# Loading the first two chunks of W and base one by one, with VectorE's first steps reordered and two warm-up products instead of five

## The chip, the core and the metric

The kernel runs on one core of a Trainium2 chip. A core has TensorE (PE, matrix products; its weight loads are listed as PEld), VectorE (DVE), ScalarE (ACT), GpSimd (POOL) and SyncE (SP), which run side by side and wait for each other through semaphores. In this kernel SP issues the loads. Sixteen DMA engines carry out every load and store. The metric is the device time of one execution in microseconds (us).

## The reference

Eight batches of x (1024 x 512 each) pass two layers with residual connections. Both are steered by a row of cond (8 x 512).

```python
# layer 0, D = 512, RANK = 8
ae = layernorm(cond) * ln_g + ln_b
h  = gelu(ae @ w1 + b1)
xw = h @ w2 + b2                       # w2: 512 x 8192
x_a, x_b = halves of xw, each reshaped to (8, 512, 8)
layer = base_layer + einsum('bdr,bkr->bdk', x_a, x_b)
x = x + (x + x @ layer)                # per batch
# layer 1
ys = cond / sqrt(512)
d  = rsqrt(ys**2 @ weight**2 + 1e-8)
x  = x + ((x * ys) @ weight) * d
```

Both layers are linear in x for a given batch, so the kernel multiplies the two matrices first and then x by the product: for batch b, with W = `weight`, P_b = (2I + base + rank part) times (I + ys W d). Float32 accuracy is reached by splitting each matrix into a rounded upper part (h) and a rest (l) and adding three products: h·h, h·l and l·h.

## The kernel before

The work has three stages. First a prologue: cond's normalisation, the layer-1 scale d, and the first matrix product (batch 0: base times W scaled by ys, tiles `pg`). Then a setup stage in which the low-rank part is made: `w2` is streamed in as sixteen tiles of 1024 KB (`w2_group`, tiles `w`, products `px` on PE), mixed with the base products of batches 1 to 3 (tiles `pq`). Then the main stage, in which each batch's x is multiplied by its matrix (tiles `po`), with the matrices of later batches made in between (tiles `pp`).

A matrix of 512 rows lies in SBUF as four chunks k of 128 rows, 128 partitions x 4 x 512. The order on PE, ACT, DVE and SP in the prologue and the setup stage is written out by hand: `mm` and `turn` pin PE's instructions, and the wrappers `ve`, `se` and `sy` pin those of DVE, ACT and SP to the order in which the code names them. So a line that moves in the code moves in the engine's queue.

The pieces that the change touches:

- Lines 86 to 92, SP's first loads: `sm` (small constants, the identity, cond transposed), cond, then W and base in two halves, then w1. In the trace these loads are `w_sb<-in_weight` (W), `b_raw<-in_baseT` (base) and `w_sb<-in_w` (this is w1; its tile's name is shortened to another's). Behind them on SP stand the w2 tiles, with consts (`cst`) after the first of them; the rows `condrows` and `b2rows` and the matrix `b_nat` come later in the stream. At most nine tiles of the pool `big` exist at a time, so a later w2 tile's load waits until PE has used up an earlier one. DMA semaphores are used in turn, eight of them, so a load also waits for the landing of the one eight before it.
- `round_yw(k)`: ACT writes the upper part of chunk k of ys·W into `nh`. `rest_yw(k)`: DVE writes the rest into `nl`.
- `twice_i(k)`: DVE adds 2I to a 128 x 128 block of base chunk k. `round_b(k, lo, hi, by)`: the upper part of columns lo to hi of base chunk k into `bh`, by ACT or, for the block of chunk 0 that `twice_i` changed, by DVE. `rest_b(k)`: DVE writes the rest into `bl`.
- `square_w(k)`: ACT squares W's chunk into `wsq`, for the products `pq_v`, from which d comes.
- `keep_warm(count)`: PE multiplies zeros by zeros, with no use of the result; 12 at the start (`WARM`), and 5 more on line 256, after the four turns of ae (`pa`) and before the first twelve products of `pg`.

After line 256 PE runs chunk 0's twelve products (four of bh·nh, four of bh·nl, four of bl·nh), then chunk 1's for two of the four tiles `pg`, then `pq_v`, then chunk 1's other two, and so on. The eleventh `w2_group` on PE stands on line 753, behind the turns `pb` of `rank_t`.

Of the kernel before, what the change touches and what calls it, by code (L numbers as in the profile page):

```python
# [14 lines left out]
P = 128  # L15
NB = 8
NT = 1024
D = 512
# [12 lines left out]
def cond_resid_kernel(ctx: ExitStack, tc: tile.TileContext, small, cond, condrows, consts,  # L31
# [12 lines left out]
    def mm(*args, **kw):  # L44
        tc.keep_in_program_order(nc.tensor.matmul(*args, **kw))  # L45

    def turn(*args):
        tc.keep_in_program_order(nc.tensor.transpose(*args))
# [36 lines left out]
    cnd, ae, xab, drow = scr[:NB, 0, :], scr[:NB, 1, :], scr[:, 2, :], scr[:, 3, :]  # L85
    sy.dma_start(sm, small)
    sy.dma_start(cnd, cond)
    for at in (slice(0, 2), slice(2, 4)):
        sy.dma_start(w_sb[:, at, :], weight[:, at, :])
        sy.dma_start(b_raw[:, at, :], baseT[:, at, :])  # L90
    w1_sb = big_tile("w1_sb")
# [14 lines left out]
    def keep_warm(count):  # L106
        for _ in range(count):
            mm(warm.rearrange("p (a c) -> p a c", c=P), zero,
               zero.unsqueeze(1).to_broadcast([P, D // P, P]), start=True, stop=True)
# [29 lines left out]
    def round_yw(k):  # L139

        se.mul(n0[k][0], w_sb[:, k, :], ysT[:, k, 0:1])

    def rest_yw(k):
        h, l = n0[k]
        ve.scalar_tensor_tensor(l, w_sb[:, k, :], ysT[:, k, 0:1], h.bitcast(F32),
                                           ALU.mult, ALU.subtract)

    def twice_i(k):
        blk = b_raw[:, k, k * P:(k + 1) * P]
        ve.scalar_tensor_tensor(blk, ident, 2.0, blk, ALU.mult, ALU.add)  # L150

    def round_b(k, lo=0, hi=D, by=se.copy):
        (by(bh[:, k, lo:hi], b_raw[:, k, lo:hi]))

    def rest_b(k):
        ve.tensor_sub(bl[:, k, :], b_raw[:, k, :], bh[:, k, :].bitcast(F32))
# [26 lines left out]
    rstd = sp.tile([NB, 1], F32, name="rstd")  # L183
    ve.tensor_mul(rstd, r, t)
    ve.tensor_scalar(ae, cnd, mv[:, 0:1], rstd, ALU.subtract, ALU.mult)
    round_yw(1)
    twice_i(0)
    round_b(0, 0, P, ve.tensor_copy)
    round_b(0, P, D)
    twice_i(1)  # L190
    round_b(1)
    rest_yw(0)
    rest_b(0)
    rest_yw(1)
    rest_b(1)
    for k in range(KC):
# [56 lines left out]
    pa = misc.tile([P, KC, NB], F32, tag="misc", name="pa")  # L253
    for k in range(KC):
        turn(pa[:, k, :], ae[:, k * P:(k + 1) * P], ident[:NB, :NB])
    keep_warm(5)
    for i, (s, m) in enumerate(((bh, n0[0][0]), (bh, n0[0][1]), (bl, n0[0][0]))):
        for c in range(KC):
            mm(pg[c], s[:, 0, c * P:(c + 1) * P], m, start=(i == 0), stop=False)
# [679 lines left out]
```

## Time and profile before

| What | Value |
|---|---|
| Median of 4 runs | 304.24 us (304.16 to 304.5) |
| Profiled execution, in all | 304.26 us |
| Its span | 302.3 us |
| PE busy | 296.1 us, 98% of the span |
| DVE busy / ACT busy / POOL busy | 177.6 / 145.6 / 34.9 us |
| Granted PE clock over the span | 0.999 |
| Bytes moved | 62.11 MB, mean 205 GB/s |
| W's two loads, issue to landing (shortest, longest) | 4.0 and 6.9 us |
| base's two loads, issue to landing (shortest, longest) | 4.9 and 7.7 us |

Times in the trace count from the start of the span. A line of the timeline or of the chain gives a start, a duration, the engine, the line of the code and what is written and read; a bracket at the end tells how long the engine sat idle before and what it waited for. Since helpers record nearly every instruction, most have line 45 (PE) or 62 (the others), and one goes by the names of tiles. A line of the stage table gives the stretch, its length, then busy time and count for PE, PEld, DVE, ACT and POOL, the granted clock, the DMA engines' busy share and GB/s. A line of the list of waits gives the waiting engine and tile, what it waited for, the sum, the number and the longest, in us.

### The profile page before, as it was taken

How to read it: one execution, taken by the hardware profiler on the slowest of the kernel's cores; microseconds unless marked ns; L12 is line 12 of the kernel's file. 1: busy time of each engine (PE TensorE's matmuls, PEld its weight loads, DVE VectorE, ACT ScalarE, POOL GpSimd, SP SyncE). 2: the span in 40 equal slices, each digit the busy share in tenths (PEclk: the TensorE clock that was granted, in tenths of full speed). 3: DMA queues.
4: the chain of work that ended last, by engine and by line, in shares of the span. 5: the costliest groups of instructions: out<-in, count | busy, mean ns of one | idle time of the engine just before them, and what ended most of it. 6: DMA issues, size and time to landing. Idle time of an engine off the chain costs nothing.

```text
span 302.3 us, 3652 instructions
## 1 busy us (share of the span) xinstructions
PE 296.1 (98%) x1369; PEld 223.4 (74%) x1369; DVE 177.6 (59%) x263; ACT 145.6 (48%) x212; POOL 34.9 (12%) x74
## 2 busy tenths in 40 slices
PE   8999999999999999999999999999999999999995
PEld 3655465466878778888888877888888878888884
DVE  4779840979569889793157549993365268500000
ACT  4756132256566672673366534664464456521221
POOL 0011000057014504100000027000000000000000
PEclk9999999999999999999999999999999999999999
DMA  6999999596519977186134348524254253522222
GB/s 203 407 430 415 407 428 415 206 329 182 194 69 324 324 244 257 72 255 211 57 112 167 112 180 207 197 88 192 60 202 184 77 208 88 228 104 104 104 85 92
DMA packets 19218, 62.11 MB, mean 205 GB/s; under 512 B 2800, under 2 KB 3312, under 8 KB 14848
## 3 DMA queue, kind: packets, MB, share of 16 engines
q1 hardware_dynamic: 6064, 38.78, 34.6%
q10 hardware_dynamic: 9360, 16.78, 14.8%
q0 software_dynamic: 3776, 6.31, 7.5%
q8 instruction: 11, 0.18, 0.3%
q14 instruction: 7, 0.06, 0.1%
HBM read 44.02 MB, written 17.84 MB: 205 GB/s over the span
## 4 chain that ended last, share of the span: by engine, by line
PE 86%; DMA 5%; DVE 5%; ACT 2%; issue 1%; SPq 0%; ACTq 0%
PE po L45 58%; PE pp L45 13%; PE pq L45 7%; DMA w<-in_w 4%; PE px L45 3%; PE pg L45 2%; DVE n L62 2%; DMA b_raw<-in_baseT 2%; PE pr L45 1%; PE pt_t L45 1%; ACT work L62 1%; DVE scr L62 0%; PE ps_t L45 0%; DVE q L62 0%; SPq L62 0%
## 5 line engine op out<-in xcount | busy, mean ns | idle before, releaser
L45 PE MATMUL po<-ph,xs 128*128 128x512 f32 (+1 forms) x520 | 165.0, 388 | 0.0
L45 PEld LDWEIGHTS po<-ph,xs 128*128 128x128 f32 x520 | 97.2, 188 | 21.5 <-issue 1.7
L45 PE MATMUL po<-pl,xs 128*128 128x512 f32 (+1 forms) x260 | 100.4, 386 | 0.0
L62 ACT COPY o<-po 128x512 f32<-128x512 f32 (+1 forms) x65 | 37.7, 580 | 85.3 <-PE po L45 85.3
L45 PEld LDWEIGHTS po<-pl,xs 128*128 128x128 f32 x260 | 48.9, 188 | 9.8
L62 DVE TENSOR_TENSOR xs<-x,xs 128x1024 fp32r<-128x1024 f32 x32 | 38.9, 1222 | 18.7 <-ACT xs L62 18.7
L62 ACT CAST xs<-x 128x1024 fp32r<-128x1024 f32 x32 | 33.4, 1053 | 3.5 <-DMA x<-in_x 3.0
L62 DVE TENSOR_TENSOR nl_p<-n,nh_p 128x1024 fp32r<-128x1024 f32 x14 | 17.1, 1223 | 23.1 <-ACT nh_p L62 23.0
L62 DVE TENSOR_TENSOR q<-pr,q 128x512 f32<-128x512 f32 x32 | 20.1, 686 | 7.0 <-PE pr L45 7.0
L509 POOL DMA_DIRECT2D fa<-kept_a x28 | 13.8, 516 | 77.3 <-PE pr L45 77.1
L62 DVE TENSOR_TENSOR pl<-q,ph 128x1024 fp32r<-128x1024 f32 x16 | 19.3, 1221 | 1.1 <-ACT ph L62 1.0
L45 PE MATMUL pq<-nh,bh 128*128 128x512 f32 x48 | 19.8, 412 | 0.0
L45 PE MATMUL pq<-nl,bh 128*128 128x512 f32 x48 | 19.1, 397 | 0.1
L45 PE MATMUL pq<-nh,bl 128*128 128x512 f32 x48 | 18.9, 394 | 0.0
L62 ACT COPY q<-pp 128x512 f32<-128x512 f32 x20 | 11.8, 588 | 14.1 <-PE pp L45 13.3
L62 DVE SCALAR_TENSOR_TENSOR n<-w_sb,ysT,d 128x512 f32<-128x512 f32 x24 | 17.8, 749 | 0.9 <-DMA d<-d_out 0.9
L62 ACT CAST ph<-q 128x1024 fp32r<-128x1024 f32 x16 | 16.6, 1052 | 3.4 <-DVE q L62 3.1
L62 ACT CAST nh_p<-n 128x1024 fp32r<-128x1024 f32 x14 | 14.7, 1052 | 3.5 <-DVE n L62 1.9
L45 PE MATMUL px<-w,hT 128*32 128x512 f32 x128 | 16.0, 601 | 0.2 <-DMA w<-in_w 0.2
L45 PEld LDWEIGHTS pq<-nh,bh 128*128 128x128 f32 x48 | 9.0, 188 | 8.4 <-issue 5.0
L509 POOL DMA_DIRECT2D ft<-kept_t x28 | 13.8, 523 | 5.0 <-DMA kept_t<-st_t 5.0
L45 PE MATMUL pp<-nh_p,sh 128*128 128x512 f32 x32 | 12.4, 389 | 0.0
(139 smaller groups left out, 285.9 us busy)
## 6 DMA issues: line engine op xcount, KB each, us to landing
w<-in_w SPq DMA_DIRECT2D x16, 1024.0 KB, 10.8
x<-in_x SPq DMA_DIRECT2D x16, 1024.0 KB, 5.3
out<-o ACTq DMA_DIRECT2D x63, 256.0 KB, 2.0
ft<-kept_t POOLq DMA_DIRECT2D x28, 64.0 KB, 3.1
fa<-kept_a POOLq DMA_DIRECT2D x28, 64.0 KB, 3.1
d<-d_out POOLq DMA_DIRECT2D x6, 256.0 KB, 3.8
w_sb<-in_weight SPq DMA_DIRECT2D x2, 512.0 KB, 5.5
b_raw<-in_baseT SPq DMA_DIRECT2D x2, 512.0 KB, 6.3
```

The lines of the kernel that those rows point to most:

```text
L45: tc.keep_in_program_order(nc.tensor.matmul(*args, **kw))
L62: return lambda *a, **kw: pin(f(*a, **kw)) if InOrder.on else f(*a, **kw)
L509: nc.gpsimd.dma_start(fold[name, b][32 * c:32 * c + 32, :], kept[name, g][32 * i:32 * i + 32, :])
```

## The change

W and base's chunks 0 and 1 are loaded by four DMAs of 256 KB (W 0, base 0, W 1, base 1) instead of two of 512 KB; chunks 2 and 3 stay together. On ACT the rounding of base chunk 0 moves ahead of that of W chunk 1. On DVE the two rests of chunk 0 move ahead of `twice_i(1)`. Of the zero products on line 256 two are left.

```diff
-    for at in (slice(0, 2), slice(2, 4)):
+    for at in (slice(0, 1), slice(1, 2), slice(2, 4)):
         sy.dma_start(w_sb[:, at, :], weight[:, at, :])
         sy.dma_start(b_raw[:, at, :], baseT[:, at, :])
...
-    round_yw(1)
+    round_b(0, P, D)
     twice_i(0)
     round_b(0, 0, P, ve.tensor_copy)
-    round_b(0, P, D)
+    round_yw(1)
+    rest_yw(0)
+    rest_b(0)
     twice_i(1)
     round_b(1)
-    rest_yw(0)
-    rest_b(0)
     rest_yw(1)
     rest_b(1)
...
-    keep_warm(5)
+    keep_warm(2)
     for i, (s, m) in enumerate(((bh, n0[0][0]), (bh, n0[0][1]), (bl, n0[0][0]))):
```

## The prediction

> **What bounds the kernel now.** I read the page's engine shares first, then the chain of work that ended last, then the waits of TensorE (PE), then the two places that these name.
>
> ```profile
> PE 296.1 (98%) x1369; PEld 223.4 (74%) x1369; DVE 177.6 (59%) x263; ACT 145.6 (48%) x212; POOL 34.9 (12%) x74
> ...
> PE 86%; DMA 5%; DVE 5%; ACT 2%; issue 1%; SPq 0%; ACTq 0%
> ```
>
> PE is busy for 98% of the span, so time can come only from places where PE waits. The list of PE's waits has four rows:
>
> ```profile
> PE warm L45 <- DVE eps_l L62: 1.0, 1, 1.0
> PE pd L45 <- DVE dst L62: 0.5, 1, 0.5
> PE pg L45 <- DVE bh L62: 0.4, 1, 0.4
> PE px L45 <- DMA w<-in_w: 0.2, 1, 0.2
> ```
>
> Row 3 is the place that the change works on. The chain over the first 12 us shows what stands before it: the load of base chunks 0 and 1, two VectorE (DVE) steps, then the products of pg.
>
> ```profile
> 1.99 4.88 DMA b_raw<-in_baseT
> ...
> 6.89 0.30 DVE b_raw L62
> ...
> 7.22 0.24 DVE bh L62
> 7.46 0.14 issue
> 7.60 4.44 PE pg L45 x18
> ```
>
> Row 4 looks harmless at 0.2 us, but it is a second gate. The chain between 30 and 50 us and PE's timeline there:
>
> ```profile
> 37.03 10.89 DMA w<-in_w
> 47.92 0.04 issue
> 47.96 1.07 PE px L45 x8
> ```
> ```profile
> 47.11 0.66 PE L48 MATMUL pb<-sm,work 128*128 128x128 f32 x4
> 47.96 1.07 PE L45 MATMUL px<-w,hT 128*32 128x512 f32 x8 [0.20 <-DMA w<-in_w]
> ```
>
> PE is ready at 47.76 and the eleventh w2 tile lands at 47.92. A transfer of 1024 KB that takes 10.89 us stands in a queue, and the stage table shows a full one:
>
> ```profile
> 2.50:4.50 2.00, 2.00 (x6) 0.72 (x5) 1.45 (x7) 0.29 (x1) 0.00 (x0) 1.00 0.86 203
> 4.50:6.00 1.50, 1.50 (x10) 0.66 (x9) 0.89 (x4) 0.36 (x1) 0.00 (x0) 1.00 0.99 396
> 6.00:7.70 1.70, 1.28 (x6) 0.46 (x7) 0.77 (x4) 1.42 (x4) 0.00 (x0) 1.00 1.00 267
> 12.00:20.00 8.00, 8.00 (x51) 4.94 (x54) 4.77 (x18) 4.62 (x10) 0.75 (x2) 1.00 1.01 422
> ...
> 40.00:45.00 5.00, 5.00 (x30) 2.72 (x29) 1.86 (x3) 1.95 (x4) 0.00 (x0) 1.00 1.02 424
> ```
>
> The last two columns are the DMA engines' busy share and GB/s. The trace's landing records agree. Each load ends on its slowest DMA engine: W chunks 0-1 at 5.62, base 0-1 at 6.87, W 2-3 at 9.36, base 2-3 at 10.61, w1 at 13.07, the first w2 tile at 15.58; and at the end the ninth w2 tile at 40.48, the tenth at 42.96, b_nat at 45.45, the eleventh at 47.92. The late steps are 2.47 to 2.49 us, which is eight packets of 8 KB at their 309 ns: that engine never rests. From 13.07 to 47.92 are 34.85 us: twelve such tiles (11 w2 and b_nat, 29.8), consts 0.36, condrows 0.65, b2rows 1.27, the d rows 1.4 and one instruction fetch about 1.35, together 34.8. There is no hole in it. So the gate at 47.92 is set by the bytes queued ahead of it, not by when PE frees a tile.
>
> **Part 1: the loads.** W chunk 0 lands earlier, as 256 KB instead of 512. Its first packet should start at 2.57 as now. W's packets of 4 KB averaged 278 ns between 2.5 and 4.5 us (base's, from 4.5 to 6.0, 163). Half the bytes are 1.1 us, and the tail to landing is now about 0.8 (5.62 less 2.57 less eight packets at 278), so W chunk 0 lands at about 4.5. Base chunk 0 is eight packets of 2 KB at 85 ns (the median of the 2 KB packets in this trace): 5.2 instead of 6.87. W 1 and base 1 land at about 6.3 and 7.0.
>
> The price: 32 packets of 2 KB per DMA engine take the place of 16 of 4 KB. At 85 against 159/2 ns that is 32 x 5.5 = 0.18, taken as 0.2 us, on a queue without holes, so everything behind lands 0.2 later, the eleventh w2 tile too. SP issues two more DMAs, 0.35 to 0.43 us and a step of about 0.45 each, so w1 is issued at 4.4 instead of 3.50 and the w2 tiles behind it as much later. That is hidden: w1's packets cannot start before base 2-3's end near 9. The semaphores of the loads go round in eight, so the third w2 tile's issue now waits for W chunk 1 and the fourth's for base chunk 1 (about 7.0, now 6.89), and consts' for W chunk 0; behind these waits on SP stand only loads whose turn comes after 15 us. If that cover were gone, it would be 0.9 us.
>
> Base 0-1 lands 1.25 us behind W 0-1, the time of its eight packets (8 x 159 ns = 1.27): loads queued behind each other pay for their packets alone. The Trainium skill, "DMA: Bandwidth & Descriptors", speaks against this part: its section "Rules for kernel authors" asks for at least 1 MiB per DMA, and "Anatomy of one DMA — SWDGE (gpsimd) path" gives each DMA a fixed cost of about 2.0 us. Two more DMAs at that price, one after the other, would be an estimate of 4 us, 308.3; the row just named gives none of it.
>
> **Part 2: the order on DVE and ScalarE (ACT).** ACT: rounding of W 0 at 4.5 to 5.2 (0.71), base 0's upper part from base's landing to about 5.75 (0.51). DVE: the row of ae ends at 5.49, then twice_i (0.29) and the copy (0.23) to 6.05, plus 0.15 to PE: 6.2. Then nl (0.74) to 6.85 and bl (0.68) to 7.55, both before PE needs them (start plus 0.93 and plus 1.9). Moved behind them: twice_i(1) at 7.55 to 7.85 (now 7.37 to 7.65), so ACT's rounding of base 1 ends at about 8.45 instead of 8.30, and the four squares at about 10.7 instead of 10.54. PE asks for the squares 4.36 us after its start (11.96 less 7.60), at about 10.7: a tie, price 0 to 0.4.
>
> **Part 3: the zeros.** PE ends the turns of ae as now; two products at 0.22 apart follow from 5.92, so PE is free at 6.36 instead of 7.0. PE's products of pg then start at about 6.36 instead of 7.60: a lead of 1.24, of which the tie leaves about 1.1. The new gap before pg is small; the old one, 0.42, left the granted clock at 1.00.
>
> **The sum.** PE would reach the eleventh px group at 47.76 less 1.1 = 46.65. Its tile lands at 47.92 plus 0.2 = 48.1. PE waits 1.45 instead of 0.20, and the rest of the program, some 254 us, starts 0.2 later than now. After this gate no wait of PE is listed, so nothing gives back or takes more. Span 302.3 + 0.2 = 302.5. The profiled execution took 304.26 in all, 2.0 around its span and 0.02 above the median of 304.24: forecast 304.45.
>
> The unknown is how W's packets fare when cut to 2 KB. The slowness follows W: 278 ns in 2.5 to 4.5, and again 245 between 6.0 and 7.7 when W 2-3 comes. In W 0-1 it cost about 8 x 108 = 0.86 us per DMA engine. No row shows 2 KB pieces of this matrix. From below: if W interleaved with base were not slowed at all, the queue would gain 0.86 and pay 0.2: 0.66 earlier. From above: if each packet, not each byte, carries the 108 ns, W 0-1 costs 16 x 108, 0.87 more, and with the 0.2 it is 1.07 later. I take the slowdown as one of bytes, nearest to W 2-3's row, which repeats it at a like rate; the range keeps both ends.
>
> **Rivals.**
> *Slower: the stall is per packet.* Place: W 0 and 1 on the DMA queue; price 1.07 in full, 305.3. It decides as slower (over 0.6 us) from a mean of about 165 ns for W's 2 KB packets. For it: the slow packets scatter from 205 to 687 ns beside many at 159, like single hits. Against: the engines' totals for W 0-1 lie within 0.74 us (first landing 4.88, last 5.62).
> *Faster: the lead reaches the end.* Then the gate would have to open early too. Should the queue be ahead by 0.66, the gate opens at 47.26 and the time is 303.6; should the lead of 1.1 come through whole, 303.1. For it: 0.2 us is a small wait, and the slowest DMA engine lost 1.35 us at one instruction fetch (the next slowest is at 47.26), which may fall elsewhere. Against: the chain without holes.
> *The loads do not come apart*, and base chunk 0 lands near 6.2: PE's lead shrinks to 0.5. The gate hides this as well: still about 304.45.
>
> **How the numbers follow.** About 0.2% (0.6 us) is what a measurement of this kernel can tell from no change. The gate holding with a shift of at most 0.6, the third rival included: 0.58, 304.45. Slower, mostly the per-packet stall: 0.25. Faster, the early gate or the whole lead: 0.17. The range leaves out about a tenth at each end: below 303.4 the lead come through nearly whole, above 305.2 the full per-packet price. So 303.4 to 305.2; the likeliest case alone spans 303.9 to 304.8.
>
> **What would show it.** Right: base chunk 0 lands near 5.2; pg's first product starts near 6.4; PE's wait for w before the eleventh px group grows from 0.2 to about 1.4; that tile lands near 48.1 and PE's order behind it is unchanged. The step on W is wrong if its 2 KB packets average well off 139 ns. All of it is wrong if PE passes the eleventh px group before 47.5, or if a wait appears after it.

## The result and the profile after

| | before | after |
|---|---|---|
| Median (lowest to highest) | 304.27 us (304.03 to 304.94), 66 runs | 304.59 us (303.83 to 306.24), 46 runs |
| Runs above 305 us | 0 of 66 | 11 of 46 |
| Profiled execution / its span | 304.26 / 302.3 us | 303.96 / 301.8 us |
| Last product of PE ends (trace) | 298.54 us | 298.65 us |
| From there to the span's end | 3.74 us | 3.20 us |

After against before the ratio is 1.0012, with an interval of 1.0007 to 1.0018: 0.3 us slower, where 0.2 was forecast. The changed kernel also scatters more, upwards above all. The profiled execution is among its shorter ones, 0.6 below the median, so its trace shows where PE waits, but not the size of the median's loss.

PE's waits after, to be read against the four rows of before (waiting tile, what it waited for, sum, number, longest, us):

```profile
PE px L45 <- DMA w<-in_w: 1.1, 1, 1.1
PE warm L45 <- DVE eps_l L62: 1.0, 1, 1.0
PE pd L45 <- DVE dst L62: 0.5, 1, 0.5
PE pa L48 <- DVE scr L62: 0.4, 1, 0.4
```

The wait of `pg` for base (0.4) is gone and the wait of `px` for a w2 tile has grown from 0.2 to 1.1. The row of `pa` is new in the list, but its turns start as before (5.56 against 5.58). The first chain of after, where base's load stood before:

```profile
5.56 0.41 PE pa L48 x4
5.97 0.54 PE warm L45 x2
6.51 0.05 issue
6.56 4.42 PE pg L45 x18
```

No load of W or base is in it any more (the chain now begins with the small load `sm`): PE goes from the turns through two products of zeros into `pg`, at 6.56 instead of 7.60. The chain between 30 and 50 us, and PE's timeline at its end:

```profile
36.04 11.83 DMA w<-in_w
47.87 0.04 issue
47.92 1.06 PE px L45 x8
```
```profile
46.16 0.66 PE L48 MATMUL pb<-sm,work 128*128 128x128 f32 x4
47.92 1.06 PE L45 MATMUL px<-w,hT 128*32 128x512 f32 x8 [1.10 <-DMA w<-in_w]
```

The eleventh w2 tile was issued 0.99 us earlier (36.04 against 37.03), and landed after 11.83 instead of 10.89: at 47.87 against 47.92. Both kernels go on at 47.92 to 47.96. The stage table after (last columns: granted clock, DMA share, GB/s):

```profile
2.50:4.50 2.00, 2.00 (x7) 0.75 (x6) 1.44 (x7) 0.29 (x1) 0.00 (x0) 1.00 0.74 142
4.50:6.00 1.50, 1.13 (x9) 0.52 (x7) 1.04 (x5) 0.81 (x2) 0.00 (x0) 1.00 1.00 361
...
40.00:45.00 5.00, 5.00 (x30) 2.59 (x28) 2.14 (x3) 1.80 (x3) 0.00 (x0) 1.00 1.02 421
```

The first stretch moved 142 GB/s instead of 203, the second 361 instead of 396; the queue at 40 to 45 is as full as before.

### The profile page after: what moved, and what is told of

It is laid out like the page before. It is cut to its first block, busy times and chain, and to the rows that moved or that the text cites. A ratio compares the mean times of both kernels' runs of the same rounds, so it can differ in the third digit from the quotient of the medians.

```text
span 301.8 us, 3650 instructions
## 1 busy us (share of the span) xinstructions
PE 295.1 (98%) x1366; PEld 222.9 (74%) x1366; DVE 178.0 (59%) x263; ACT 145.5 (48%) x212; POOL 35.7 (12%) x74
## 4 chain that ended last, share of the span: by engine, by line
PE 85%; DMA 6%; DVE 6%; ACT 2%; issue 1%; ACTq 0%
PE po L45 58%; PE pp L45 13%; PE pq L45 6%; DMA w<-in_w 6%; PE px L45 3%; PE pg L45 2%; DVE n L62 2%; PE pr L45 1%; DMA sm<-in_small 1%; PE pt_t L45 1%; DVE scr L62 1%; ACT work L62 1%; DVE q L62 0%; PE pq_v L45 0%; ACT nh L62 0%
```

## The experiments

Theory A: the lead that PE wins at `pg` ends at the eleventh w2 tile, which lands when the DMA queue lets it. Rival B: the lead is lost elsewhere. Rival C: it is the order on DVE or the missing zeros that cost the 0.3 us. Each comparison is with the kernel before on the same chip, whose medians were 304.20 (first four), 304.53 (next four), 304.31 (next three) and 304.19 (last). On two of these chips the kernel before itself had 2 runs of 29 above 305 (highest 305.22 and 305.10).

| Kernel | Runs | Median (lowest to highest) | Ratio to before, interval |
|---|---|---|---|
| changed, b_nat late | 12 | 304.18 (303.24 to 305.07) | 1.0000 (0.9988 to 1.0012) |
| before, b_nat late | 11 | 304.19 (303.98 to 304.30) | 1.0000 (0.9992 to 1.0009) |
| loads alone | 6 | 305.62 (304.96 to 306.94) | 1.0050 (1.0033 to 1.0068) |
| order and zeros alone | 12 | 304.20 (303.79 to 305.18) | 1.0005 (0.9996 to 1.0014) |
| W cut alone | 12 | 304.63 (304.07 to 307.66) | 1.0021 (0.9998 to 1.0044) |
| changed, W 0-1 whole | 12 | 304.31 (303.23 to 305.31) | 0.9990 (0.9978 to 1.0003) |
| changed, six zeros | 12 | 304.61 (303.81 to 306.30) | 1.0006 (0.9992 to 1.0021) |
| W 0-1 whole, b_nat late | 5 | 303.36 (303.27 to 303.78) | 0.9966 (0.9953 to 0.9979) |
| changed, base 2-3 first | 11 | 303.90 (303.73 to 304.50) | 0.9985 (0.9976 to 0.9993) |
| W 0-1 whole, b_nat late, again | 12 | 303.83 (303.12 to 304.45) | 0.9985 (0.9975 to 0.9995) |
| order and zeros, b_nat late | 11 | 304.09 (303.98 to 304.32) | 0.9989 (0.9980 to 0.9997) |
| W 0-1 whole, b_nat late, base 2-3 first | 7 | 303.41 (303.28 to 303.94) | 0.9977 (0.9965 to 0.9988) |

**Is PE's path slack? Six zeros instead of two, in the changed kernel.**

```diff
-    keep_warm(2)
+    keep_warm(6)
```

> The changed kernel with six products of zeros in place of two (4 x 0.22 = 0.88 us more work on PE ahead of pg). Theory A: PE has a slack of 1.1 us at the eleventh w2 tile, so the wait there shrinks to about 0.2 and the time stays that of the changed kernel, 304.4 to 304.7. Rival (PE's path sets the end): 0.9 more, 305.4.

PE's timeline of this kernel at both places:

```profile
6.08 1.47 PE L45 MATMUL warm<-zero 128*128 128x512 bf16 x6
7.45 1.16 PE L45 MATMUL pg<-nh,bh 128*128 128x512 f32 x4
```
```profile
47.62 0.66 PE L48 MATMUL pb<-sm,work 128*128 128x128 f32 x4
48.40 1.06 PE L45 MATMUL px<-w,hT 128*32 128x512 f32 x8
```

`pg` starts 0.89 later than in the changed kernel (7.45, 6.56), and the median is the same, 304.61 against 304.59. The two were measured on different chips, but the ratio to the kernel before, 1.0006 (0.9992 to 1.0021), has no room for the 0.9 us (0.3%) more that a PE-bound start would cost. The tile landed at 48.35 here, and the profiled time is 304.46, 0.50 above that of the changed kernel; its tile landed 0.48 later. In this one trace PE came only 0.12 ahead of its start at the tile (48.28, 48.40), so it is the medians that part the two: the time follows the tile and not PE's start, A, and a PE-bound start is out.

**Take the gate away: b_nat's load behind the eleventh w2 tile, in both kernels.**

```diff
-        if len(todo) == 6:
+        if len(todo) == 5:
```

> The changed kernel with one more edit: b_nat's load (1024 KB) is issued behind the eleventh w2 tile instead of ahead of it, so that this tile should land one tile's time (2.47 us) earlier, near 45.4 us. Theory A (PE's lead of about 1.0 us is lost at the eleventh w2 tile): PE's wait of 1.10 there is gone, the whole rest of the program moves up by about 1.1, time 303.5. Rival B (the lead is lost elsewhere, the wait at the tile is only where it shows): PE waits at another place behind and the time stays at 304.4 to 304.6.

> The kernel before with the same edit: b_nat's load behind the eleventh w2 tile. Theory A: PE came to that tile at 47.76 and waited 0.20, so no more than 0.2 to 0.3 is to be had here: 304.0 to 304.1, about 0.6 to 0.9 over the changed kernel with the same edit. Rival B: both kernels gain the same from this edit.

The kernel before gained nothing that can be told (304.19 where A allowed 304.0 to 304.1). The changed kernel was expected at 303.5 and came to 304.18, though four of its twelve times are 303.24 to 303.59 (no trace of one of these was kept). PE's timeline of its profiled execution (304.9) shows a second loss:

```profile
8.79 1.10 PE L45 MATMUL pg<-nh,bl 128*128 128x512 f32 x4
10.76 0.50 PE L45 MATMUL pg<-nh,bh 128*128 128x512 f32 x1 [0.87 <-ACT bh L62]
```
```profile
48.09 0.66 PE L48 MATMUL pb<-sm,work 128*128 128x128 f32 x4
48.67 1.07 PE L45 MATMUL px<-w,hT 128*32 128x512 f32 x8
```

The eleventh tile landed at 46.45 and PE found it there, so the gate is gone; but the lead was already lost before 11 us. PE waited 0.87 for base chunk 1. Twelve of the sixteen DMA engines had landed their part of it by 7.37, the other four came at 8.33, 8.64, 9.35 and 9.74. Theory A was incomplete: the cut loads bring late DMA engines, which hold PE up directly and, through the queue, the w2 tiles.

**Which part brings the late engines?** The loads of the change alone:

> The kernel before with the loads of the change alone (W 0, base 0, W 1, base 1 singly; old order of VectorE and ScalarE, five products of zeros). ScalarE then rounds W 1 before base 0 and PE's first pg product should start at about 7.9. Theory A: PE comes to the eleventh w2 tile within 0.3 of the kernel before, the tile lands where the 2 KB packets put it: 304.5 to 304.7, and single runs scatter upwards as in the changed kernel (up to 306). Rival C (the order on VectorE or the missing zeros cost the 0.3 us): 304.2 to 304.3, scatter as in the kernel before.

The order and the zeros alone, with the loads in pairs:

> The kernel before with the order on VectorE and ScalarE and the two products of zeros of the change, but W and base in pairs of chunks as before. pg starts at 7.6 as before (base lands at 6.87); the squares end near 12.1, PE may wait up to 0.3 for them. Theory A: 304.2 to 304.5, and single runs scatter no more than in the kernel before (304.0 to 304.9). Rival C: 304.6, with the changed kernel's scatter.

W's chunks 0 and 1 singly, base 0-1 whole, old order:

> The kernel before with only W's chunks 0 and 1 loaded singly, one behind the other; base 0-1 stays one load, and the order on the engines stays. Theory W (W's packets of 2 KB carry the stalls): W 1 ends late on some DMA engines, the stream behind it as well, 304.6 to 305.6 with single runs up to 306. Theory M (it is the mixing of W and base chunks in turn, or base's cut, that lets DMA engines drift apart): base 0-1 lands at 6.9 to 7.1 and the time is 304.2 to 304.4.

W's chunks 0 and 1 whole, base 0 and base 1 singly, in the changed kernel:

> The changed kernel with W's chunks 0 and 1 in one load again; base 0 and base 1 singly behind it. Base 0 should land near 6.25, pg start near 7.0, a lead of 0.6 that is lost at the eleventh w2 tile. Theory W: no stalls beyond the kernel before's, tile at 47.9 to 48.0, 304.2 to 304.4, scatter as in the kernel before. Theory M or base's cut: 304.6 or more, with the changed kernel's scatter.

Order and zeros alone cost nothing that can be told in the median, which speaks against C. The interval's upper end, 1.0014, still holds the changed kernel's 1.0012, but the same order and zeros with b_nat late, below, lie at 0.9989. That they add scatter is not excluded: three of the twelve times, 304.69 to 305.18, lie above all 29 of the kernel before on that chip (highest 304.65), and none had been expected above 304.9. The loads alone cost 1.4 us, well over the 0.3 to 0.5 expected: in the old order `twice_i(1)` stands ahead of chunk 0's rests on DVE, so a late base chunk 1 (last engine 9.23) stops PE after chunk 0's first four products:

```profile
8.04 0.97 PE L45 MATMUL pg<-nh,bh 128*128 128x512 f32 x3 [0.28 <-ACT bh L62]
10.27 1.21 PE L45 MATMUL pg<-nl,bh 128*128 128x512 f32 x4 [1.26 <-DVE nl L62]
```

and its eleventh tile landed at 50.69, where PE waited 1.31 more. By the medians the new order (on DVE and ACT) saves about 1 us once the loads are cut (305.62 against 304.59, on different chips). This trace alone doesn't show that: the tile sets its end, and its last DMA engine came 1.51 behind the fifteenth (49.18), after an instruction fetch at 46.47. With W cut alone the interval still touches 1, but four of twelve times are 305.45 to 307.66; the profiled one, 307.35, shows PE's start held by base 0-1, whose sixteen engines landed between 6.35 and 9.05 (6.20 to 6.87 before):

```profile
5.96 1.25 PE L45 MATMUL warm<-zero 128*128 128x512 bf16 x5
9.77 1.17 PE L45 MATMUL pg<-nh,bh 128*128 128x512 f32 x4 [2.56 <-DVE bh L62]
```

With base alone cut the median is 0.2 below the kernel before's (the interval holds 1), and the scatter remains: in its profiled execution, 305.29, base 1's engines landed between 6.71 and 9.41. So either cut can bring late engines.

**Is it base 1 beside W 2-3?** In the four traces above whose base came late, the late load is base's last piece ahead of W 2-3. It is not the only spread one: W 0 as a load of 256 KB landed over 1.34 to 2.45 us in six traces, W 0-1 as one load over 0.60 to 1.02 in the eight others, and with W cut alone most of the spread (2.45 of 2.70) was there from W 0 on. The changed kernel with base 2-3 ahead of W 2-3:

```diff
-    for at in (slice(0, 1), slice(1, 2), slice(2, 4)):
+    for at in (slice(0, 1), slice(1, 2)):
         sy.dma_start(w_sb[:, at, :], weight[:, at, :])
         sy.dma_start(b_raw[:, at, :], baseT[:, at, :])
+    sy.dma_start(b_raw[:, 2:4, :], baseT[:, 2:4, :])
+    sy.dma_start(w_sb[:, 2:4, :], weight[:, 2:4, :])
```

> The changed kernel with base 2-3 loaded ahead of W 2-3. Theory S (the late DMA engines come from base 1 being read while other engines already read W 2-3): base 1's last landing stays within about 1 us of its first, W 2-3 lands near 10.7, PE waits up to 1.2 for the squares (hidden by its slack of 1.1 at the eleventh w2 tile), time 304.0 to 304.4, single runs no more than 305. Theory W (the 2 KB packets stall by themselves, whatever stands behind them): base 1 or W 1 still spreads over 2 us in most runs, 304.6 to 305.5 with runs up to 306.

303.90, 0.15% below the kernel before, and no time above 304.5: a scatter of 0.8 us instead of 2.4 (11 runs against 46, on different chips), with as many small packets. Base 1 landed between 6.38 and 7.57; the changed kernel's own trace, from one of its shorter runs, has 6.59 to 7.56, so it is the scatter that speaks here. The price shows on ACT, where the squares wait for W 2-3, as expected:

```profile
8.57 1.15 ACT L62 ACTIVATE wsq<-w_sb 128x512 f32<-128x512 f32 x2
10.93 1.15 ACT L62 ACTIVATE wsq<-w_sb 128x512 f32<-128x512 f32 x2 [1.21 <-DMA w_sb<-in_weight]
```

**Base cut, with the gate moved.** W 0-1 whole, base 0 and 1 singly, new order, two zeros, b_nat late; its repetition; its control without base's cut; and with base 2-3 first as well:

> The kernel with W 0-1 in one load, base 0 and 1 singly (as in the kernel named before with base cut alone), and b_nat's load behind the eleventh w2 tile. Theory A with theory W: pg starts near 7.0, no wait at the eleventh tile, lead of 0.6 reaches the end: 303.6 to 303.8, faster than both kernels. If DMA engines stall with base's cut too: 304.0 to 304.5.

> The kernel with W 0-1 in one load, base 0 and 1 singly and b_nat's load behind the eleventh w2 tile, once more, since its five times may have missed the late DMA engines that the same loads had in the run with base cut alone. If the gain holds: 303.3 to 303.6. If late engines are as frequent here: single runs up to 304.5, median 303.6 to 304.

> The order and the two zeros of the change with W and base in pairs as before, and b_nat's load behind the eleventh w2 tile: the control for the kernel with base cut, whose lead comes from base 0 landing early. Here pg starts at 7.55 as before, there is no lead to bring to the end, and PE comes to the tile as in the kernel before: 304.0 to 304.2. If the late b_nat load alone gave the gain: 303.4.

> The kernel with base cut and b_nat late (W 0-1 in one load, base 0 and 1 singly), now with base 2-3 loaded ahead of W 2-3. Theory S: base 1 lands on all DMA engines within about 1 us (7.2 at the latest, 8.07 and 8.36 without the swap) and single runs scatter by less than 0.8 instead of 1.3; pg starts near 7.0; the squares of W 2 and 3 end near 12 and take back all but 0.2 to 0.4 of the lead, so the median is 303.8 to 304.1. If the spread stays over 1.3: base 1 is late for another reason than W 2-3 beside it.

All three versions lie below the kernel before, but the first one's gain halved on another chip (0.34%, then 0.15%), with times up to 304.45. The control is 0.1% below the kernel before, within its expected times, and its interval overlaps that of the repetition on the same chip. The last version has 303.41, a ratio of 0.9977 (0.9965 to 0.9988), and a scatter of 0.7 us. Its chain at the old gate is PE alone:

```profile
45.84 0.99 PE px L45 x8
46.83 0.59 PE pb L48 x4
47.42 0.99 PE px L45 x8
```

It came out better than the 303.8 to 304.1 expected through the end of the program, told below: that is 0.47 shorter here, and 303.41 plus 0.47 is 303.88.

The same end is in the other gains, and it is no gain of PE's. Medians against the kernel before on the same chip, and what is left of them when the shorter end of the version's one trace is taken off (worked out, us):

| Kernel | Below before | Shorter end | Left for PE |
|---|---|---|---|
| W 0-1 whole, b_nat late | 1.17 | 0.45 | 0.72 |
| again, on another chip | 0.48 | 0.46 | 0.02 |
| and base 2-3 first | 0.78 | 0.47 | 0.31 |
| order and zeros, b_nat late (control) | 0.22 | 0 | 0.22 |
| changed, base 2-3 first | 0.41 | 0.55 | -0.14 |
| changed, b_nat late | 0.02 | 0.56 | -0.54 |

So a lead of PE's at the end of the program stands on five runs, and on seven that have no control on their chip; the twelve of the repetition don't have it in the median. In the traces PE's last product ends at 297.96, 298.09 and 298.05 in the three versions, at 298.54 in the kernel before and at 298.31 in the control, but also at 298.05 with order and zeros alone, where nothing was cut. That cutting base pays through PE is not settled.

The last version's base 1 still landed between 6.33 and 7.93, not by 7.2: keeping W 2-3 away went with narrower times, but W 2-3 is not the whole cause of late engines. What makes a single DMA engine late stays open; packets of 2 KB that took 1082 ns in the changed kernel and 1566 in the one with b_nat late (median 84) were seen, not explained.

## Why the prediction was right, and where its steps were not

The forecast 304.45 met 304.59 and the named mechanism was shown: PE's lead is won and then waited away at the eleventh w2 tile. But that the sum of +0.2 came out near the truth is luck: two errors of opposite sign, +0.7 and -0.4, nearly cancel.

- **Base 0 at 5.2, `pg` at 6.36**: 5.83 and 6.56. W 0 landed at 5.17, not 4.5: its first DMA engine was done at 3.55 and its last 1.62 later, where half of W 0-1's transfer had been counted with W 0-1's spread of 0.74. The lead was 1.04 instead of 1.24, the wait at the tile 1.10 instead of 1.45. As the gate swallows both, this cost nothing.
- **The tie at the squares, 0 to 0.4**: none. `pq_v` starts 4.35 us after `pg`, as before (4.36).
- **Packet cost 0.2**: w1 landed at 13.21 against 13.07, 0.14, in this trace, where w1's sixteen engines landed within 1.49 (1.23 before). Two more loads cost nothing like the estimate of 4 us here. The Trainium skill gives the price of 2.0 us ("DMA: Bandwidth & Descriptors", "Anatomy of one DMA — SWDGE (gpsimd) path") for DMAs on GpSimd's path. These loads are issued by SP, so no run here tests that price where the page states it.
- **The queue later by 0.2 in all: the step that failed.** In the profiled execution the tile was 0.05 earlier, which is no measure of the step. An instruction fetch of 16 KB fell on the fourth w2 tile before (24.74 on its last engine, 1.35 behind the fifteenth) and on the fifth after (27.11, 1.11 behind). From there the queue after stood ahead, by 0.25 at b_nat (45.20 against 45.45), and lost 0.20 of that at the eleventh tile. In the median the tile is later: the changed kernel's median lies 0.63 above that profiled execution, and the time follows the tile, so the tile lands near 48.5, 0.6 later than before. That is worked out, not seen; with six zeros and the same loads it was seen at 48.35. What the sum has no term for is that DMA engines come late. w1 landed between 13.41 and 15.11 in the four other traces with all four cut loads, between 12.37 and 13.08 in the four traces with pairs.
- **The rival "the stall is per packet"** is not what came. The mean of W's 2 KB packets, which was to decide it at 165 ns, is about 136 in the changed kernel and 136 to 156 in those four other traces (all 512 packets of 2 KB, less 256 for base at the median of 84; worked out), near the 139 foretold. The mean held, the spread did not: the prediction leaned on engines' totals within 0.74 us, and W 0 alone was spread over 1.62. 11 of 46 runs exceed 305; no trace of such a run of this kernel is kept, so that late engines make them is argued from the other kernels' traces.
- **"After this gate nothing takes more"**: not quite. The sixteenth w2 tile landed at 62.83 instead of 62.59, and PE's products for it began 0.16 later than before (62.88 against 62.72), where PE had been 0.05 ahead just before (62.35 against 62.40). The list of waits doesn't show it, but it is a wait behind the gate, which the prediction had named as a sign of being wrong, and the 0.2 lost at it is as large as the loss that was forecast.
- **The end of the program: a term not seen.** It was taken as unchanged, but is 0.54 shorter. At the end SP waits on the eight DMA semaphores in a fixed order, and two more loads move the last output's DMA from the first of the five shown waits to the third (times of SP's instructions from the two traces):

```
semaphore          106      107      108      109      110      drain    last output lands
before  SP at   300.70   300.78   301.23   301.31   301.37     301.45    300.68 (on 106)
after   SP at   298.86   299.50   300.82   300.88   300.95     301.01    300.81 (on 108)
```

From landing to drain are 0.77 us before and 0.20 after; 0.45 of it is one step between two waits whose semaphores were long met. All fourteen traces agree: PE's last product to the span's end is 3.74 to 3.76 with no load added (four kernels), 3.28 to 3.35 with one (five), 3.19 to 3.20 with two (five). So the median's +0.3 is about +0.7 at PE's last product (304.59 less 5.31, against 304.27 less 5.72; the profiled executions' times from PE's end on) and -0.4 behind it.

The rival "the lead reaches the end" did not come true in the changed kernel; with the gate moved and W whole it did in part in the first five runs, and hardly in the median of the twelve that repeated them.

## What to carry to other kernels

A wait of 0.2 us in the list can be a gate: before paying for an earlier start, ask which later wait ends on something that the start doesn't move, here a queue without holes, and move that first. Cutting the first load to start sooner was paid on the DMA engines here: each load ends with the slowest of sixteen, and the smaller pieces landed further apart, so compare scatter as well as medians. And count what stands behind the last product: a load more or less changed the program's end by as much as the gains in question, so take that off before crediting a gain to the start.

## What the runs showed of the hardware that was not expected

- One DMA engine of sixteen landed its part of a 256 KB load up to 3.6 us after the first (base 1 in the changed kernel with b_nat late, 6.13 to 9.74), while base 0-1 as one load of 512 KB behind W 0-1 had a spread of 0.67 us (kernel before).
- The program's end shortened by 0.4 to 0.55 us when one or two loads were added near its start, by the place of the last output's semaphore in SP's closing waits.
- An instruction fetch of 16 KB took 1.09 us on its DMA engine (kernel before, at 22.44), and the w2 tile that was being loaded then landed on its last engine at 24.74, 1.35 us behind the fifteenth; in the changed kernel the fetch came at 24.95, that tile had landed on all sixteen by 23.53, and it was the next one whose last engine (27.11) came 1.11 behind the fifteenth.
